# Keys turned by VectorE and moved by DMA, and two chunks in one score run, in a fused transformer block

## The chip, the cores and the metric

The kernel runs on one core of a Trainium2 chip. The metric is the device time of one execution, in microseconds (us). All arithmetic is in float32. The names used below: TensorE (PE) multiplies matrices and writes to PSUM, VectorE (DVE) and ScalarE (ACT) work on elements, GpSimd (POOL) does some element work in SBUF, SyncE (SP) issues nearly all DMAs.

## The reference, cut to what matters

x is 2 x 2048 x 256. Six modulation rows come from silu(c) and a matrix. Then, per token:

```
h = layernorm(x) * (1 + ca) + sa
q, k, v = split(h @ W_attn + b)              # 16 heads of 16 channels
phi(z) = exp(z @ omega - |z|^2 / 2) / sqrt(128)   # 128 features, z scaled by 1/4
S_t = sum over s <= t of phi(k_s) v_s^T ;  Z_t = sum over s <= t of phi(k_s)
y_t = phi(q_t) S_t / (phi(q_t) Z_t + 1e-6)   # causal linear attention
x = x + ga * (y @ W_proj + b_proj)
h = layernorm(x) * (1 + cb) + sb
x = x + gb * FFN(h)     # 4 experts, top 2, one shared base and a rank-4 part each
```

## The kernel before

**Tiles.** The 4096 tokens are eight blocks of 512 (`N = 8`, four per batch row). A block has four head groups g of four heads j and four chunks t of 128 tokens. Attention inside a chunk is a masked product of features; across chunks a running state `S[g]` carries the sums.

**Features.** `query_key` projects one 128-channel quarter n (0, 1 queries; 2, 3 keys), adds the bias on VectorE into `qs`, squares it on ACT, and SP writes both halves to DRAM (`qd`). `reload` reads one group's four heads back as `f`. `features` multiplies f by omega in four 32-row tiles (`pp`, four PSUM banks), `exponentials` makes `phi` on ACT, 128 features on the partitions and 512 tokens along the row, one tile for each head and side (side 1 is keys).

**Attention.** For every chunk the kernel does four things:

- `keys` turns the chunk's key features with four 128x128 transposes on TensorE (L413) into a PSUM bank `pk`; `keep_keys` copies the bank to SBUF (`kt`) on ACT (L421). `kt` has tokens on the partitions.
- `scores` (L431) makes the scores with 16 matmuls on 32-column groups of the array into the bank `pa`. The four matmuls of a round are of equal length and belong to four different heads (head j = c XOR u), so rows of `pa` hold blocks of 32 tokens in an order that depends on the head. VectorE multiplies the bank by `causal` into `am` (L437).
- `outputs` uses `kt` and v for the state's increment `ps` (L455, 16 matmuls), am and v for the part inside the chunk (L459) and S and phi for the part before it (L462). VectorE adds the increment to S (L471) and copies the 128x128 result to `y` (L475).
- Because of the order of tokens in `pa`, key features are written with their 32-token blocks exchanged (`quarters` in `exponentials`), and `values` computes v in 32-token pieces (L358), 64 instructions a chunk. v has 32 columns a head: 16 values and 16 ones, the ones giving the denominator.

**Order.** A loop runs over blocks i and eight pair steps k; step k handles two chunks. The written order of each engine is kept (`keep_written_order`), so what stands ahead of an instruction on its engine runs first. A step is: `run_full` (full-width TensorE work of other blocks), keys of two chunks, `scores` of the second chunk, `outputs` of the first, `features` of a later group, `amid` (VectorE work and DMAs of other blocks), exponentials, values, `scores` of the next step's first chunk, `outputs` of the second chunk, `behind`. `run_full`, `amid` and `behind` put the other stages of blocks i+1, i-1 and i-2 into fixed steps:

| step k | TensorE in run_full | VectorE and DMAs in amid and behind |
|---|---|---|
| 0 | channels1 (L283), hidden and first, query_key | divide_invert: den, rdr, inv |
| 1, 2 | hidden and first (L660, L646), query_key (L318), second (L646, g on L687) | step 2: divide (L515) |
| 3 | project (L522), its norm2_stats | norm2 (L273) |
| 4 | channels2 (L283), finish (L694) | |
| 5 | finish; router after scores | choose, norm1_stats |
| 6 | finish, low_rank (L618) | norm1 |
| 7 | weigh (L632, h on L637), finish, hidden and first, query_key, second | divide_load: den, num |

The FFN units (`hidden`, `first`, `second`) of a block begin in step 7 of the block after it and go on in steps 0 to 2 of the next, so they are missing in block 0 and in steps 0 to 2 of block 1, and the `finish` pieces are missing in blocks 0 and 1. The last block's FFN runs after the loop.

`divide_invert` writes the inverted denominators to DRAM (`rdr`, L503) and reads them back spread over partitions (`inv`, L506); `divide` multiplies num by inv; `project` needs its result. The SP queue issues its DMAs in the written order.

**PSUM.** Eight banks: `pa`, `pk`, `s` and five of the rotating tag `mm`.

Of the kernel before, what the change touches and what calls it, by code (L numbers as in the profile page):

```python
# [14 lines left out]
P = 128  # L15
NH = 16
# [16 lines left out]
def kernel(  # L33
# [32 lines left out]
    HW = 2 * DH  # L66
    CH = 8
# [91 lines left out]
    tri = work.tile([P, P], FP, tag="am", name="tri")  # L159
    make_upper_triangular(nc, tri, val=1.0, diag=True)  # L160
    causal = const.tile([P, HG, P], FP, name="causal")
    for c in range(4):
        for j in range(HG):
            nc.vector.tensor_copy(
                causal[c * CG : (c + 1) * CG, j, :], tri[(c ^ j) * CG : ((c ^ j) + 1) * CG, :]
            )

    pa = psum.tile([P, TB], FP, tag="pa", name="pa", bufs=1)
    nc.vector.memset(pa, 0.0)
# [144 lines left out]
    def query_key(i, n):  # L314
        s = st[i]
        pq = mm_tile(f"pq{i}_{n}")
        for k in range(KC):
            nc.tensor.matmul(  # L318
                pq, w_sb[:, k, n * P : (n + 1) * P], s["hT"][:, k, :],
                start=(k == 0), stop=(k == KC - 1),  # L320
            )


        tag = {1: "num", 3: "h2"}.get(n, "qs") if i == 0 else "qs"
        qs = work.tile(
            [P, 2, TB], FP, tag=tag, name=f"qs{i}_{n}", bufs=2 if tag == "qs" else 1
        )
        nc.vector.tensor_scalar(  # L328
            qs[:, 0, :], pq, bqk[:, n : n + 1], 1.0 / math.sqrt(DH), ALU.add, ALU.mult
        )  # L330
        nc.scalar.activation(qs[:, 1, :], qs[:, 0, :], AF.Square)
        qd = dram.tile([2 * HG, 2, DH, TB], FP, tag="qd", name=f"qd{i}_{n}", bufs=4)
        nc.sync.dma_start(qd[:, 0], qs[:, 0, :])
        if i == 0:
            nc.scalar.dma_start(qd[:, 1], qs[:, 1, :])
        else:
            nc.sync.dma_start(qd[:, 1], qs[:, 1, :])
        s["qd"][n] = qd

    def reload(i, n, hf):  # L340
        side, g = divmod(2 * n + hf, NG)
        f = work.tile([P, TB], FP, tag=f"f{side}{g}", name=f"f{i}_{side}{g}", bufs=1)
        nc.sync.dma_start(f, st[i]["qd"][n][hf * HG : (hf + 1) * HG].rearrange("j s d t -> (j s d) t"))
        st[i]["feat"][side, g] = f

    def values(i, t):

        s = st[i]
        if t == 0:
            s["v"] = work.tile([P, NT, NH, HW], FP, tag="v", name=f"v{i}")  # L350
            nc.gpsimd.memset(s["v"][:, :, :, DH:HW], 1.0)
        pv = mm_tile(f"pv{i}_{t}")
        wv = w_sb[:, :, 2 * C : 3 * C].rearrange("p k (g j d) -> p k j g d", j=HG, d=DH)
        for j in range(HG):
            for k in range(KC):
                for c in range(4):
                    t0 = t * P + (c ^ j) * CG
                    nc.tensor.matmul(  # L358
                        pv[c * CG : (c + 1) * CG, j * HG * DH : (j + 1) * HG * DH],
                        s["hT"][:, k, t0 : t0 + CG], wv[:, k, j],  # L360
                        start=(k == 0), stop=(k == KC - 1),
                    )
        nc.vector.tensor_add(
            s["v"][:, t, :, 0:DH].rearrange("p (g j) d -> p j g d", j=HG),
            pv[:, 0:C].rearrange("p (j g d) -> p j g d", j=HG, d=DH),
            bv_bc[:].rearrange("p (g j d) -> p j g d", j=HG, d=DH),
        )


    S, phi, turned, staged, y = {}, {}, {}, {}, {}  # L370

# [12 lines left out]
    def quarters(ap, j):  # L384

        n, b = {1: (2, CG), 2: (2, 2 * CG), 3: (4, CG)}[j]
        return ap.rearrange("p (a n b) -> p a n b", n=n, b=b)

    def exponentials(i, g, side, pps):
        for j in range(HG):  # L390
# [3 lines left out]
            if side and j:  # L394

                nc.scalar.activation(  # L396
                    quarters(ph[:], j)[:, :, ::-1], quarters(pps[j][:], j), AF.Exp, bias=lnm
                )
            else:
                nc.scalar.activation(ph, pps[j], AF.Exp, bias=lnm)  # L400
# [6 lines left out]
    def keys(i, g, t, bank=None):  # L407

        if not carried(i, t):
            return  # L410
        pk = bank or psum.tile([P, TB], FP, tag="pk", name=f"pk{i}_{g}{t}", bufs=1)
        for j in range(HG):
            nc.tensor.transpose(  # L413
                pk[:, j * P : (j + 1) * P], phi[i, g, 1, j][:, t * P : (t + 1) * P], ident
            )
        turned[i, g, t] = pk

    def keep_keys(i, g, t):
        if (i, g, t) in turned:
            kt = work.tile([P, HG, M], FP, tag="kt", name=f"kt{i}_{g}{t}")  # L420
            nc.scalar.copy(kt[:].rearrange("p h m -> p (h m)"), turned[i, g, t])  # L421
            turned[i, g, t] = kt

    def scores(i, g, t):

        q, k = ([phi[i, g, side, j] for j in range(HG)] for side in range(2))
        ts = slice(t * P, (t + 1) * P)
        for u in range(4):
            for c in range(4):
                j, t0 = c ^ u, t * P + c * CG  # L430
                nc.tensor.matmul(  # L431
                    pa[c * CG : (c + 1) * CG, j * P + u * CG : (j + 1) * P],
                    k[j][:, t0 : t0 + CG], q[j][:, t * P + u * CG : (t + 1) * P],
                    start=True, stop=True,
                )
        am = work.tile([P, HG, P], FP, tag="am", name=f"am{i}_{g}{t}")
        nc.vector.tensor_mul(am, pa[:].rearrange("p (h q) -> p h q", h=HG), causal)  # L437
        staged[i, g, t] = am

    def outputs(i, g, t):  # L440

        ts = slice(t * P, (t + 1) * P)
        am, kt = staged.pop((i, g, t)), turned.pop((i, g, t), None)
        fresh = i % NBLK == 0 and t == 0
        bank = psum.tile([P, TB], FP, tag="s", name=f"ps{i}_{g}{t}", bufs=1)
        ps, py = (bank[:, n * P : (n + 1) * P] for n in range(2))
        vs = [st[i]["v"][:, t, g * HG + j, :] for j in range(HG)]
        rows = [slice(j * HW, (j + 1) * HW) for j in range(HG)]  # L450
        if kt is not None:
            for j in range(HG):
                for c in range(4):
                    cg = slice(c * CG, (c + 1) * CG)
                    nc.tensor.matmul(  # L455
                        ps[cg, rows[j]], kt[:, j, cg], vs[j], start=True, stop=True
                    )
        for j in range(HG):
            nc.tensor.matmul(py[rows[j], :], vs[j], am[:, j, :], start=True, stop=fresh)  # L459
        if not fresh:  # L460
            for j in range(HG):
                nc.tensor.matmul(  # L462
                    py[rows[j], :], S[g][:, rows[j]], phi[i, g, 0, j][:, ts],
                    start=False, stop=True,
                )
        if kt is not None:
            new = work.tile([P, P], FP, tag=f"S{g}", name=f"S{i}_{g}{t}")
# [5 lines left out]
        if t == 0:  # L473
            y[g] = work.tile([P, TB], FP, tag="y", name=f"y{i}_{g}")
        nc.vector.tensor_copy(y[g][:, ts], py)  # L475
        if t == NT - 1:
# [254 lines left out]
    for n, hf in ((2, 0), (0, 0), (2, 1), (0, 1)):  # L731
        reload(0, n, hf)
    query_key(0, 3)
    query_key(0, 1)
    for n, hf in ((3, 0), (1, 0), (3, 1), (1, 1)):
        reload(0, n, hf)
# [4 lines left out]
    for g, side in ((0, 1), (0, 0)):  # L741
        exponentials(*features(0, g, side))
    keys(0, 0, 0)
    keep_keys(0, 0, 0)
    scores(0, 0, 0)
    exponentials(*features(0, 1, 1))
# [47 lines left out]
    def amid(i, k):  # L794
# [9 lines left out]
        if a < N:  # L804
            for kk, n, hf in (
                (1, 2, 0), (1, 2, 1), (2, 0, 0), (2, 0, 1), (3, 3, 0), (4, 3, 1), (7, 1, 0), (7, 1, 1),
            ):
                if kk == k:
                    reload(a, n, hf)
# [24 lines left out]
    def chunk_at(n):  # L834
        i, n = divmod(n, NG * NT)
        return i, *divmod(n, NT)

    TOTAL = N * NG * NT
    for i in range(N):
        for k in range(PAIRS):  # L840
            n = (i * PAIRS + k) * 2
            run_full(i, k)
            keys(*chunk_at(n + 1))
            if n + 2 < TOTAL:
                keys(*chunk_at(n + 2), bank=mm_tile(f"pk{n + 2}"))
            keep_keys(*chunk_at(n + 1))
            scores(*chunk_at(n + 1))
            if k == 5 and i:
                router(i - 1)
            outputs(*chunk_at(n))  # L850

            gi, gg = divmod(n // NT + 1 + k % 2, NG)
            quad = features(gi, gg, k % 2) if gi < N else None
            amid(i, k)
            if n + 2 < TOTAL:
                keep_keys(*chunk_at(n + 2))
            if quad:
                exponentials(*quad)
            if 3 <= k < 7 and i + 1 < N:
                values(i + 1, k - 3)  # L860
            if n + 2 < TOTAL:
                scores(*chunk_at(n + 2))
            outputs(*chunk_at(n + 1))
# [8 lines left out]
    def other_set(name):  # L872
        return [pa, mm_tile(f"{name}0")] + [
            psum.tile([P, TB], FP, tag=tag, name=f"{name}{tag}", bufs=1) for tag in ("pk", "s")
        ]
# [89 lines left out]
```

## Time and profile before

| | us |
|---|---|
| median of 3 runs (838.94, 842.99, 842.58) | 842.58 |
| span of the profiled execution, first to last instruction | 844.1 |
| PE busy | 785.1 |
| DVE busy | 420.3 |
| ACT busy | 296.8 |
| POOL busy | 134.5 |

The profiled execution is known by its span alone; the span is 1.5 us above the median of the runs. TensorE's mean granted clock was 0.968 of full speed; it was 0.80 from 25 to 50 us, 0.86 from 50 to 100 us, 0.86 again from 150 to 175 us and from 725 to 775 us, and 1.00 nearly everywhere between. Block 0 runs from about 43 to 110 us, block 1 to 193 us, and a later block takes 93 to 97 us.

How to read a page: the busy row gives the time in which an engine had an instruction under way. The chain is followed back from the last instruction to whatever released it, so its shares are of time on the path. In the timeline each row has the start, the length, the engine, the line, the operation, its output and inputs, the shape and the number of instructions; square brackets give idle time before it and what ended it. SPq rows are DMA issues on SP; their length is the time that issuing takes.

### The profile page before, as it was taken

How to read it: one execution, taken by the hardware profiler on the slowest of the kernel's cores; microseconds unless marked ns; L12 is line 12 of the kernel's file. 1: busy time of each engine (PE TensorE's matmuls, PEld its weight loads, DVE VectorE, ACT ScalarE, POOL GpSimd, SP SyncE). 2: the span in 40 equal slices, each digit the busy share in tenths (PEclk: the TensorE clock that was granted, in tenths of full speed). 3: DMA queues.
4: the chain of work that ended last, by engine and by line, in shares of the span. 5: the costliest groups of instructions: out<-in, count | busy, mean ns of one | idle time of the engine just before them, and what ended most of it. 6: DMA issues, size and time to landing. Idle time of an engine off the chain costs nothing.

```text
span 844.1 us, 34168 instructions
## 1 busy us (share of the span) xinstructions
PE 785.1 (93%) x15536; PEld 576.6 (68%) x15536; DVE 420.3 (50%) x1183; ACT 296.8 (35%) x570; POOL 134.5 (16%) x170
## 2 busy tenths in 40 slices
PE   4898999699999999999998999999899999889888
PEld 3466667566687667766776667776677677767666
DVE  5445467644557337544556347553464335532622
ACT  1354344334434343334433344334433233311021
POOL 1000200021201122021201122021220121012223
PEclk9798899989999999999999999999999999979999
DMA  3565235104410353013500353013410220102000
GB/s 120 180 207 188 97 118 177 42 4 136 143 42 16 98 158 91 16 50 113 158 28 16 92 164 89 17 37 121 118 50 16 75 69 14 53 2 66 1 26 26
DMA packets 45392, 68.18 MB, mean 81 GB/s; under 512 B 6848, under 2 KB 20352, under 8 KB 45248
## 3 DMA queue, kind: packets, MB, share of 16 engines
q1 hardware_dynamic: 43088, 63.90, 24.3%
q8 instruction: 122, 2.00, 1.0%
q10 hardware_dynamic: 2160, 2.10, 0.8%
q14 instruction: 22, 0.18, 0.1%
HBM read 36.37 MB, written 29.62 MB: 78 GB/s over the span
## 4 chain that ended last, share of the span: by engine, by line
PE 85%; DVE 9%; issue 3%; DMA 2%; POOL 0%; ACT 0%; SPq 0%; DVEq 0%; ACTq 0%; POOLq 0%
PE ph L660 12%; PE pa L431 10%; PE pf L694 9%; PE pp L378 8%; PE pk L413 7%; PE pq L318 6%; PE ph L646 4%; PE ps L455 4%; PE ps L459 4%; PE pv L358 4%; PE po L522 4%; PE ps L462 3%; PE pf L715 2%; PE ptf L283 1%; PE pl L618 1%
## 5 line engine op out<-in xcount | busy, mean ns | idle before, releaser
L688 POOL TENSOR_TENSOR g<-g,r 128x256 f32<-128x256 f32 x128 | 90.2, 736 | 372.0 <-DVE g L687 372.0
L437 DVE TENSOR_TENSOR am<-pa,causal 128x512 f32<-128x512 f32 x128 | 88.2, 689 | 72.4 <-PE pa L431 69.0
L400 ACT ACTIVATE phi<-pp,lnm 128x512 f32<-128x512 f32 x160 | 99.5, 688 | 61.4 <-PE pp L378 61.4
L421 ACT COPY kt<-pk 128x512 f32<-128x512 f32 x120 | 69.6, 581 | 146.0 <-PE pk L413 101.5
L431 PEld LDWEIGHTS pa<-phi,phi 128*32 128x32 f32 x4096 | 87.9, 113 | 37.8 <-DVE y L475 19.7
L660 PE MATMUL ph<-h,wi_sb 128*128 128x256 f32 x448 | 105.3, 388 | 4.8 <-DVE h L637 2.6
L694 PE MATMUL pf<-wo_g,g 128*128 128x256 f32 x448 | 103.3, 384 | 0.2 <-DVE g L687 0.2
L431 PE MATMUL pa<-phi,phi 128*32 128x64 f32 (+3 forms) x4096 | 101.1, 241 | 0.7 <-DVE am L437 0.7
L660 PEld LDWEIGHTS ph<-h,wi_sb 128*128 128x128 f32 x448 | 84.4, 193 | 22.0 <-DVE h L637 3.8
L694 PEld LDWEIGHTS pf<-wo_g,g 128*128 128x128 f32 x448 | 83.1, 190 | 17.2 <-issue 7.0
L328 DVE TENSOR_SCALAR qs<-pq,bqk 128x512 f32<-128x512 f32 x32 | 24.0, 750 | 132.5 <-PE pq L318 66.4
L378 PE MATMUL pp<-f,om 32*128 32x512 f32 x512 | 79.5, 660 | 2.5 <-DVE statsa L263 2.5
L674 ACT ACTIVATE r<-ph 128x256 f32<-128x256 f32 x112 | 34.1, 389 | 128.7 <-PE ph L646 119.4
L413 PE MATMUL pk<-ident,phi 128*128 128x128 f32 x480 | 69.1, 289 | 0.5 <-DVE qs L328 0.5
L413 PEld LDWEIGHTS pk<-ident,phi 128*128 128x128 f32 x480 | 58.2, 149 | 16.4 <-issue 12.7
L455 PE MATMUL ps<-v,kt 128*32 128x32 f32 x3840 | 60.7, 200 | 6.8 <-issue 6.5
L318 PE MATMUL pq<-hT,w_sb 128*128 128x512 f32 x128 | 63.6, 623 | 0.8 <-DVE hT L286 0.7
L459 PE MATMUL ps<-am,v 128*32 128x128 f32 x1024 | 60.3, 288 | 0.9 <-DVE y L475 0.7
L396 ACT ACTIVATE phi<-pp,lnm 128x512 f32<-128x512 f32 x96 | 58.7, 688 | 0.0
L462 PE MATMUL ps<-phi,S 128*32 128x128 f32 x960 | 55.5, 278 | 3.2 <-issue 3.2
L455 PEld LDWEIGHTS ps<-v,kt 128*32 128x32 f32 x3840 | 49.9, 113 | 7.7 <-issue 7.6
L687 DVE SCALAR_TENSOR_TENSOR g<-ph,rho 128x256 f32<-128x256 f32 x112 | 39.4, 414 | 25.8 <-PE ph L646 25.8
(175 smaller groups left out, 868.7 us busy)
## 6 DMA issues: line engine op xcount, KB each, us to landing
f<-qd SPq DMA_DIRECT2D x64, 256.0 KB
qd<-qs SPq DMA_DIRECT2D x60, 256.0 KB
ydr<-y SPq DMA_DIRECT2D x32, 256.0 KB
num<-ydr SPq DMA_DIRECT2D x16, 256.0 KB
inv<-rdr SPq DMA_DIRECT2D x16, 256.0 KB
xt<-in_x_dram SPq DMA_DIRECT2D x7, 512.0 KB
out_dram<-xt SPq DMA_DIRECT2D x7, 512.0 KB
wo_g<-in_woT_dram SPq DMA_DIRECT2D x2, 1024.0 KB
```

What stands on the lines that cost most here:

```text
L318: nc.tensor.matmul(pq, w_sb[:, k, n * P : (n + 1) * P], s["hT"][:, k, :], start=(k == 0), stop=(k == KC - 1),)
L378: nc.tensor.matmul(pp, om[rs, :], f[rs, :], start=True, stop=True, tile_position=(2 * DH * j, 0))
L400: nc.scalar.activation(ph, pps[j], AF.Exp, bias=lnm)
L413: nc.tensor.transpose(pk[:, j * P : (j + 1) * P], phi[i, g, 1, j][:, t * P : (t + 1) * P], ident)
L431: nc.tensor.matmul(pa[c * CG : (c + 1) * CG, j * P + u * CG : (j + 1) * P], k[j][:, t0 : t0 + CG], q[j][:, t * P + u * CG : (t + 1) * P], ...
L437: nc.vector.tensor_mul(am, pa[:].rearrange("p (h q) -> p h q", h=HG), causal)
L455: nc.tensor.matmul(ps[cg, rows[j]], kt[:, j, cg], vs[j], start=True, stop=True)
L459: nc.tensor.matmul(py[rows[j], :], vs[j], am[:, j, :], start=True, stop=fresh)
L462: nc.tensor.matmul(py[rows[j], :], S[g][:, rows[j]], phi[i, g, 0, j][:, ts], start=False, stop=True,)
L660: nc.tensor.matmul(ph, wi_sb[:, k, f * P : (f + 1) * P], s["h2"][:, k, ts], start=(k == 0), stop=False, skip_group_check=True,)
L688: nc.gpsimd.tensor_add(g, g, r[j // 2][:, j % 2, :])
L694: nc.tensor.matmul(po[:, 0:C], s["g"][f][:, t * P : (t + 1) * P], wo_g[i // NBLK][:, f, :], start=(f == 0), stop=(f == NF - 1),)
```

## The change

- TensorE no longer turns the keys. For every group of a block, `turn_keys` runs four VectorE transposes of 128x512, each of which turns 32x32 blocks, into `kb` (one buffer), and 16 DMAs within SBUF (32 partitions x 4 x 512 bytes, 64 KB each) that put the blocks together into `kt`. `pk` is gone, and with it `keep_keys` on ACT. It is called in even steps, after the exponentials of the group's queries, for the group whose increments begin two steps later; for the very first group before the loop.
- `scores` does both chunks of a pair in one run of 32 matmuls into two banks `pa0` and `pa1`; the even chunk has its 32-token blocks in order, the odd chunk in reverse (mirrored), so that each column group gets long and short matmuls in turn and 160 columns a head in all. The order no longer depends on the head: `quarters` goes, `causal` has two planes, and `values` is two full-width matmuls a chunk. `mirror_values` makes a copy of the odd chunks' v with the blocks in reverse (`vr`), four DMAs a block, issued in step 6.
- v has 17 columns a head (`DV`), and so has the state. A step now runs: `run_full`, values, `increments` of both chunks, S on VectorE, `scores` of the next pair, `outputs` of both chunks (y copied by ACT, 128x256), `features`, exponentials, `turn_keys` in even steps, `amid`, one `reload`, `behind`.
- `qs` has one buffer where it had two, and f four where it had eight.

```diff
-        qs = work.tile(
-            [P, 2, TB], FP, tag=tag, name=f"qs{i}_{n}", bufs=2 if tag == "qs" else 1
-        )
+        qs = work.tile([P, 2, TB], FP, tag=tag, name=f"qs{i}_{n}", bufs=1)
...
+    def quad_at(n):
+        i, n = divmod(n, 2 * NG)
+        return i, n // 2, 1 - n % 2
+
+    def reload(n):
+        i, g, side = quad_at(n)
+        if i >= N:
+            return
+        m, hf = divmod(side * NG + g, 2)
+        f = work.tile([P, TB], FP, tag="f", name=f"f{i}_{side}{g}", bufs=4)
+        nc.sync.dma_start(f, st[i]["qd"][m][hf * HG : (hf + 1) * HG].rearrange("j s d t -> (j s d) t"))
+        st[i]["feat"][side, g] = f
...
         pv = mm_tile(f"pv{i}_{t}")
+        for k in range(KC):
+            nc.tensor.matmul(
+                pv[:, 0:C], s["hT"][:, k, t * P : (t + 1) * P], w_sb[:, k, 2 * C : 3 * C],
+                start=(k == 0), stop=(k == KC - 1),
+            )
...
+    def mirror_values(i):
+        s = st[i]
+        s["vr"] = work.tile([P, NT // 2, NH, DV], FP, tag="vr", name=f"vr{i}")
+        odd = s["v"][:].rearrange("p (a e) h d -> p a e (h d)", e=2)[:, :, 1]
+        for c in range(4):
+            nc.sync.dma_start(
+                s["vr"][c * CG : (c + 1) * CG].rearrange("p a h d -> p a (h d)"),
+                odd[(3 - c) * CG : (4 - c) * CG],
+            )
...
+    def turn_keys(i, g):
+        blocks = work.tile([P, NT * 4, HG, CG], FP, tag="kb", name=f"kb{i}_{g}", bufs=1)
+        for j in range(HG):
+            nc.vector.transpose(
+                blocks[:, :, j, :], phi[i, g, 1, j][:].rearrange("p (b t) -> p b t", t=CG)
+            )
+        kt = work.tile([P, NT, 4, HG, CG], FP, tag="kt", name=f"kt{i}_{g}")
+        src = blocks[:].rearrange("p (t q) j m -> p t q (j m)", q=4)
+        for q in range(4):
+            for m in range(4):
+                nc.sync.dma_start(
+                    kt[q * CG : (q + 1) * CG, :, m].rearrange("p t j m -> p t (j m)"),
+                    src[m * CG : (m + 1) * CG, :, q],
+                )
+        turned[i, g] = kt
+
+    def scores(i, g, u):
+        q, k = ([phi[i, g, side, j] for j in range(HG)] for side in range(2))
         for j in range(HG):
+            for e in range(2):
+                t0 = (2 * u + e) * P
+                for c in range(4):
+                    a = 3 - c if e else c
+                    nc.tensor.matmul(
+                        pa[e][c * CG : (c + 1) * CG, j * P + a * CG : (j + 1) * P],
+                        k[j][:, t0 + a * CG : t0 + (a + 1) * CG],
+                        q[j][:, t0 + a * CG : t0 + P],
+                        start=True, stop=True,
+                    )
+        for e in range(2):
+            am = work.tile([P, HG, P], FP, tag="am", name=f"am{i}_{g}{u}{e}", bufs=3)
+            nc.vector.tensor_mul(
+                am, pa[e][:].rearrange("p (h q) -> p h q", h=HG),
+                causal[:, e, :].unsqueeze(1).to_broadcast([P, HG, P]),
+            )
+            staged[i, g, 2 * u + e] = am
+
+    def increments(i, g, u):
+        bank = py_bank
+        kt = turned[i, g]
...
+                    nc.tensor.matmul(
+                        bank[c * CG : (c + 1) * CG, (e * HG + j) * DV : (e * HG + j + 1) * DV],
+                        kt[:, t, c, j, :], st[i]["v"][:, t, g * HG + j, :],
+                        start=True, stop=True,
+                    )
...
+        nc.scalar.copy(y[g][:, 2 * u * P : 2 * (u + 1) * P], bank[:, 2 * P : 4 * P])
...
             run_full(i, k)
-            keys(*chunk_at(n + 1))
-            if n + 2 < TOTAL:
-                keys(*chunk_at(n + 2), bank=mm_tile(f"pk{n + 2}"))
-            keep_keys(*chunk_at(n + 1))
-            scores(*chunk_at(n + 1))
+            if 3 <= k < 7 and i + 1 < N:
+                values(i + 1, k - 3)
+            increments(*pair_at(n))
+            if n + 1 < TOTAL:
+                scores(*pair_at(n + 1))
             if k == 5 and i:
                 router(i - 1)
-            outputs(*chunk_at(n))
...
+            outputs(*pair_at(n))
+            gi, gg, side = quad_at(n + 3)
+            if gi < N:
+                exponentials(*features(gi, gg, side))
+                if side == 0:
+                    turn_keys(gi, gg)
             amid(i, k)
...
```

## The prediction

> **What bounds the kernel now.** I read the page's first section, then its chain of waits, then the chain in order of time and the engines' timelines for the third of a block's eight pair steps.
>
> ```profile
> PE 785.1 (93%) x15536; PEld 576.6 (68%) x15536; DVE 420.3 (50%) x1183; ACT 296.8 (35%) x570; POOL 134.5 (16%) x170
> ...
> PE 85%; DVE 9%; issue 3%; DMA 2%; POOL 0%; ACT 0%; SPq 0%; DVEq 0%; ACTq 0%; POOLq 0%
> PE ph L660 12%; PE pa L431 10%; PE pf L694 9%; PE pp L378 8%; PE pk L413 7%; PE pq L318 6%; PE ph L646 4%; PE ps L455 4%; PE ps L459 4%; PE pv L358 4%; PE po L522 4%; PE ps L462 3%; PE pf L715 2%; PE ptf L283 1%; PE pl L618 1%
> ```
>
> TensorE ends the kernel: 85% of the chain, and the key transposes (pk, L413) are 7% of it. VectorE's 50% looks like room, but that is an average. The next two views are one step, first the chain, then what VectorE and TensorE do at its end:
>
> ```profile
> 410.51 0.65 PE ph L646 x8
> 411.15 1.02 PE pk L413 x8
> 412.18 0.69 PE pa L431 x32
> 412.87 0.28 PE ps L455 x25
> 413.15 0.32 PE ps L459 x8
> 413.47 1.07 PE pp L378 x8
> 414.54 0.69 PE pa L431 x32
> ...
> 416.00 3.65 PE po L522 x16
> ```
>
> ```profile
> 411.27 1.41 DVE L687 SCALAR_TENSOR_TENSOR g<-ph,rho 128x256 f32<-128x256 f32 x4
> ...
> 412.94 0.69 DVE L437 TENSOR_TENSOR am<-pa,causal 128x512 f32<-128x512 f32 x1 [0.27 <-PE pa L431]
> ...
> 413.95 1.83 DVE L515 TENSOR_TENSOR num<-num,inv 128x512 f32<-128x512 f32 x2
> ...
> 415.93 0.48 PE L522 MATMUL po<-wp_g,num 128*128 128x256 f32 x1
> ```
>
> The division (L515) ends at 415.78 and the projection that reads it starts at 415.93: here VectorE is on time by 0.15 us, with nothing to spare. Last, the SP queue, the start of the kernel and a block's first steps, and one row of its waits:
>
> ```profile
> 1.24 1.88 SPq L95 DMA_DIRECT2D xt<-in_x_dram  x4
> ...
> 389.01 0.60 SPq L333 DMA_DIRECT2D qd<-qs  x1
> 389.66 0.60 SPq L337 DMA_DIRECT2D qd<-qs  x1
> 391.40 0.32 SPq L503 DMA_DIRECT2D rdr<-den  x1
> 397.33 1.27 SPq L506 DMA_DIRECT2D inv<-rdr  x2
> ```
>
> ```profile
> SPq L506 <- DMA rdr<-den: 28.8, 8, 5.8
> ```
>
> Issuing one DMA holds SP for 0.32 to 0.65 us, four alike are 0.47 us apart (1.88/4), and SP waits on average 3.6 us (28.8/8) for rdr before inv, with everything behind it in line.
>
> **What it takes away.** 480 transposes, eight a step at 1.02 us: 480/8 x 1.02 = 61 us, all on the path. With them go ACT's 120 copies (69.6 us) and VectorE's 128 y copies (35.8 us; ACT now makes 64); ACT and these copies are off the path, worth nothing by themselves. TensorE's small waits for pk and its copies (0.2 to 0.5 us at 306.8, 363.1, 375.3) also go: about 0.6 us in each of seven blocks, 4 us. Gain: 65 us.
>
> **What stays equal.** Scores: 16 matmuls take 0.58 us from start to start (the 128x512 features give another rate, 1.07/512 x 320 = 0.67). A pair runs 640 columns per column group in both kernels; between a saving of 0.1 and a loss of 0.18 a step I take 0, as the nearest row is the same matmul. Values: 64 instructions at 0.92 us become 4 full-width ones; the projection's like pieces take 3.65/4 = 0.91. Increments stream 17 columns, not 32, but the router's matmuls with 20 columns (0.62 us for 64 instructions) are no faster per instruction than these (0.28 for 32): 0.
>
> **What it adds.** 128 VectorE transposes of 128x512, four in every even step (0, 2, 4, 6). No row shows one. Bounds: 0.60 us, the pitch of the am rows, and 1.25, twice that; I take 0.69, am's own duration (88.2/128), the nearest operation of that size: 2.76 us a group. 512 DMAs of 64 KB within SBUF, 16 a group, all on SP: 0.34 to 0.62 us apart by the rows above; I take 0.47, 7.5 us a group. Both sit, in their engine's order, ahead of the division, the inversion's DMAs and the next step's qd. Where that shows, step by step:
>
> (a) Step 2 into 3. VectorE from the start of L646: g done at 2.24; two S adds 0.4; two am, now both behind the whole score run, 1.22: 3.86; transposes 6.62; division 1.75: 8.4. TensorE reaches the projection after 0.65 + 0.56 (increments, two of 0.28) + 1.16 (scores, two of 0.58) + 1.05 (outputs, two of 0.22 and 0.30) + 1.07 (features) = 4.5. New stall 3.9 us, in 7 blocks: 27.
>
> (b) Step 3 into 4: the second norm's xh pieces now follow both am; 0.6 us x 7 = 4.
>
> (c) Steps 0 to 2, the SP queue. From the end of step 0's transposes: key DMAs 7.5, rdr 0.3, its wait 3.6, inv 1.3, f 0.4, then step 1's two qd 1.3: 14.4; qd lands some 2.5 later (f at 400.61 waited about so long): 16.9. qs has one buffer now, so step 2's qs on VectorE waits for that landing, and behind it queue g, S, am, transposes and the division. Cover: rest of step 0 2.1, step 1 10.7 (3.65 + 0.65 + 1.91 + 0.65 + 3.84), step 2 up to qs 6.2, less the 4.2 that VectorE needs from the scores to the transposes' end: 14.8. Late by 2.1, in blocks 2 to 6: 10.
>
> (d) Block 1 has no FFN units in steps 0 to 2, so its cover is some 9 us shorter at the throttled clock (0.86): about 9 of stall. In step 7, transposes, norm1 and h x pw (4.2 + 1.3 + 1.3) meet TensorE after 3.2 (no finish in between): 3.6. The router's chain, with the same cover missing, 1. Sum 14.
>
> (e) Block 0 is shortest, 6 to 7 us a step. The first keys need 7.5 + 2.5 us of DMA at the start: 2.4 not covered. Each later group needs 4.2 + 7.5 + 2.5 = 14.2 against 2.1 + 6.5 + 2.3 = 10.9: 3.3, three times. In step 2 qs also waits for a qd that stands behind key DMAs and eight weight loads (6 us from 48.65): about 10. Less some 4 us of waits for weights that the old kernel has here too: 18.
>
> **What else moves, at nothing.** y's copy on ACT (0.39, as the 128x256 r rows) runs under the features (1.07), before the next increments write that bank. The exponentials, now last in a step, free four banks in some 2.8 us while the next step's first 3.65 us need one bank per 0.9; without that cover, up to 1.7 a step. The four mirror DMAs a block stand behind step 6's keys and have step 7 (over 11 us) to land. The reloads, one a step, are issued two steps ahead. The other even steps fall on finish (3.65 us) or hidden (3.65), which cover 2.76 us of VectorE; without that cover they would cost up to 2.76 each. Costs 27 + 4 + 10 + 14 + 18 = 73, against 65: plus 8. The profiled execution spanned 844.1 us, 1.5 above the median of 842.58; 844.1 + 8 - 1.5 is about 850.
>
> **Two rules of the Trainium skill.** The trace has no VectorE transpose. "VectorE: DVE Perf Modes", section "The three transpose paths", gives 311 ns for VectorE on a 128x128 bf16 tile and advises TensorE for full 128x128 transposes. Four such would be 1.24 us for 128x512, an estimate from that page; (a), (c), (d) and (e) would then rise to the slow rival's sum. "DMA: Bandwidth & Descriptors", section "Measured (HBM→SBUF, 128 partitions, SWDGE, issued from GpSimd)", gives 0.95 us for 64 KB; if the key DMAs ran one after another at that, a group would take 15 us and (c) would be 7.7 us worse. No run here shows either.
>
> **Rivals.** Faster, about 823: VectorE takes 0.60 and SP issues every 0.33 us, as for one contiguous tile (f, ydr at 0.32). Then (c) is gone (7.5 - 5.3 = 2.2), (a) is 25, (d) 11, (e) about 9, (b) 4: 49 against 65, and a score run that saves 0.1 us a step adds 6: 844.1 - 22 = 822. It decides below a pitch of 0.34. For it: rows of 0.32; against: kt's pattern has three levels on both sides, and such rows take 0.39 to 0.60.
>
> Much slower, about 890: one transpose takes 1.25, so a group 2.2 us more: (a) +15, (c) +11, step 7 +13, blocks 0 and 1 +15: near 905; or the pitch is 0.62, as for qd and inv, 2.4 us more a group: (c) +12, blocks 0 and 1 +12: near 875. From one transpose of 0.8 us on, step 7 is no longer covered. Against: am and hT, of the same size, take 0.69 and 0.81.
>
> That the transposes stay on TensorE is no rival: none is left in the new program.
>
> **Numbers.** Forecast 850 (its own range 836 to 870), 0.48; about 823 (800 to 838), 0.36; about 890 (870 to 920), 0.16. The range of 8 in 10 leaves out the low end of the second and the high end of the third: 810 to 893. A measurement of this kernel can tell about 0.5% from no change, 838.4 to 846.8. Faster 0.36 (nearly all of the second case); within 0.12 (mostly the forecast's low side); slower 0.52.
>
> **What would show it.** Right: PE's busy time down by 50 to 65 us; VectorE's up to 470 to 500; a row "PE po <- DVE num" of some 25 us where it was 3.0; VectorE's qs waiting for DMA qd<-qs; increments in block 0 waiting for kt; a transpose row near 0.69 us; SP at 0.45 to 0.5 us per kt DMA. Wrong: those waits missing with the rows short (faster), or score runs well over 1.3 us a pair, which none of my cases has.

## The result and the profile after

The changed kernel takes 935.36 us in the median (931.53 to 939.99), the kernel before 842.12 on the same chip: a ratio of 1.108, interval 1.100 to 1.116. The profiled execution spans 934.4 us with a mean granted clock of 0.907, where it was 844.1 and 0.968. The forecast was 850 and the top of its range 893. Some executions of a kernel are slower at a lower granted clock; the ratios leave these out and the medians do not, which is why 900.37 us below goes with a ratio of 1.060.

The page's busy row and its chain of waits, of the changed kernel:

```profile
PE 762.0 (82%) x13136; PEld 532.9 (57%) x13136; DVE 446.4 (48%) x1174; ACT 253.8 (27%) x514; POOL 128.3 (14%) x170
...
PE 48%; DVE 16%; SPq 15%; DMA 13%; issue 5%; ACT 1%; DVEq 0%; POOL 0%; ACTq 0%
SPq L424 12%; DMA qd<-qs 9%; PE ph L687 9%; PE pf L721 8%; PE pp L395 5%; DVE kb L417 4%; PE po L549 4%; PE pa L438 3%; DVE g L714 3%; PE py_bank L493 3%; PE pq L322 3%; PE ph L673 2%; PE py_bank L496 2%; PE py_bank L462 2%; PE pf L742 2%
```

TensorE carried 85% of the chain and now carries 48%. Its first line is no matmul: it is SP issuing the key DMAs (L424, 12%), then the landing of qd (9%). TensorE is idle for 934.4 - 762.0 = 172 us, where it was 59.

Next, two group rows (instructions, busy time, mean ns of one, idle time ahead) and three rows of waits (us, times, longest), of the changed kernel:

```profile
L330 DVE TENSOR_SCALAR qs<-pq,bqk 128x512 f32<-128x512 f32 x32 | 24.0, 751 | 226.9 <-DMA qd<-qs 151.8
...
L417 DVE STREAM_TRANSPOSE kb<-phi 128x512 f32<-128x512 f32 x128 | 79.4, 677 | 2.2 <-ACT phi L406 2.2
```

```profile
DVE qs L330 <- DMA qd<-qs: 151.8, 12, 21.4
...
PE py_bank L493 <- DVE S L478: 82.0, 26, 11.0
...
PE po L549 <- DVE num L542: 8.1, 8, 2.6
```

VectorE's turning costs what was taken for it (0.677 us, forecast 0.69). The large row is qs waiting for the transfer that still reads its one buffer. TensorE does not show that wait under its own name: it waits for S, which stands behind qs in VectorE's order. The stall that was forecast to be dearest, the projection behind the division, is the 8.1.

One such wait from end to end. First SP's timeline of block 4, steps 0 to 2, of the changed kernel, then the chain over the same time:

```profile
463.11 11.67 SPq L424 DMA_DIRECT2D kt<-kb  x16
474.88 1.75 SPq L530 DMA_DIRECT2D rdr<-den  x1
477.79 1.32 SPq L533 DMA_DIRECT2D inv<-rdr  x2
479.17 0.44 SPq L353 DMA_DIRECT2D f<-qd  x1
479.71 0.61 SPq L335 DMA_DIRECT2D qd<-qs  x1
480.42 0.61 SPq L339 DMA_DIRECT2D qd<-qs  x1
```

```profile
477.79 0.64 SPq L533
478.49 0.63 SPq L533
479.17 0.44 SPq L353
479.71 0.61 SPq L335
480.42 8.98 DMA qd<-qs
...
490.19 1.41 DVE g L714 x4
...
493.35 2.48 DVE kb L417 x4
495.83 0.58 DVE num L542
496.46 5.96 PE po L549 x16
```

Sixteen issues take 11.67 us; behind them stand the inversion and step 1's qd, which lands (has arrived, so that its source is free) at 489.40, 8.98 us after the start of its issue. VectorE starts qs at 489.52, after 18.07 us of idling, and then works off what is queued behind it: g, S, am, transposes, division. The projection follows at 496.46 and takes 5.96 us where it took 3.65. The landing itself, by windows of the changed kernel (length, busy us of PE, PEld, DVE, ACT and POOL, granted clock, DMA share, GB/s):

```profile
474.90:480.40 5.50, 5.50 (x129) 3.19 (x131) 0.00 (x0) 1.21 (x4) 0.00 (x0) 1.00 0.23 66
480.40:489.40 9.00, 0.67 (x38) 0.50 (x28) 0.00 (x0) 0.00 (x0) 0.00 (x0) 0.70 0.77 232
```

In nine microseconds TensorE works for 0.67. The DMA engines are busy: 9.0 us x 232 GB/s is 2.1 MB, the transfers that SP lets go at once. In this stretch the mean clock granted is 0.70; in windows of it, it is 1.00 up to 482 us, while TensorE still has work, and 0.64 from 482 to 489.

Where in the kernel the time went: from step 0 of one block to step 0 of the next (the start of the first hT on VectorE), blocks 0 to 5 took 67.8, 82.0, 94.3, 92.7, 97.3 and 94.6 us before, and 90.7, 109.2, 101.1, 106.7, 105.1 and 105.2 after. Blocks 0 and 1 lose 23 and 27 us, later blocks 7 to 14.

### The profile page after: what moved, and what is told of

The parts are those of the page before. It is cut to its first block, busy times and chain, and to the rows that moved or that the text cites. A ratio compares the mean times of both kernels' runs of the same rounds, so it can differ in the third digit from the quotient of the medians.

```text
span 934.4 us, 29993 instructions
## 1 busy us (share of the span) xinstructions
PE 762.0 (82%) x13136; PEld 532.9 (57%) x13136; DVE 446.4 (48%) x1174; ACT 253.8 (27%) x514; POOL 128.3 (14%) x170
## 2 busy tenths in 40 slices
DMA packets 121667, 103.74 MB, mean 111 GB/s; under 512 B 15552, under 2 KB 96640, under 8 KB 121536
## 4 chain that ended last, share of the span: by engine, by line
PE 48%; DVE 16%; SPq 15%; DMA 13%; issue 5%; ACT 1%; DVEq 0%; POOL 0%; ACTq 0%
SPq L424 12%; DMA qd<-qs 9%; PE ph L687 9%; PE pf L721 8%; PE pp L395 5%; DVE kb L417 4%; PE po L549 4%; PE pa L438 3%; DVE g L714 3%; PE py_bank L493 3%; PE pq L322 3%; PE ph L673 2%; PE py_bank L496 2%; PE py_bank L462 2%; PE pf L742 2%
## 5 line engine op out<-in xcount | busy, mean ns | idle before, releaser
L438 PE MATMUL pa<-phi,phi 128*32 128x128 f32 (+3 forms) x4096 | 96.8, 245 | 9.1 <-issue 9.1
L721 PEld LDWEIGHTS pf<-wo_g,g 128*128 128x128 f32 x448 | 84.8, 194 | 26.8 <-issue 11.4
L493 PE MATMUL py_bank<-am,v 128*17 128x128 f32 x512 | 31.1, 299 | 82.9 <-DVE S L478 82.0
L502 ACT COPY y<-py_bank 128x256 f32<-128x256 f32 x64 | 23.7, 371 | 250.9 <-PE py_bank L496 225.4
L395 PE MATMUL pp<-f,om 32*128 32x512 f32 x512 | 87.6, 736 | 5.1 <-DVE xha L277 4.7
L438 PEld LDWEIGHTS pa<-phi,phi 128*32 128x32 f32 x4096 | 85.0, 116 | 11.5 <-issue 9.9
L417 DVE STREAM_TRANSPOSE kb<-phi 128x512 f32<-128x512 f32 x128 | 79.4, 677 | 2.2 <-ACT phi L406 2.2
L462 PEld LDWEIGHTS py_bank<-v,kt 128*32 128x32 f32 x3840 | 44.4, 114 | 49.7 <-issue 37.1
L462 PE MATMUL py_bank<-v,kt 128*32 128x17 f32 x3840 | 52.7, 189 | 22.8 <-DMA kt<-kb 22.8
L496 PE MATMUL py_bank<-phi,S 128*17 128x128 f32 x960 | 58.0, 296 | 8.9 <-issue 8.9
L493 PEld LDWEIGHTS py_bank<-am,v 128*17 128x17 f32 x512 | 12.0, 100 | 89.5 <-DVE S L478 89.4
L333 ACT ACTIVATE qs<-qs 128x512 f32<-128x512 f32 x32 | 20.2, 632 | 147.4 <-DVE qs L330 147.4
```

The source lines that it names most:

```text
L395: nc.tensor.matmul(pp, om[rs, :], f[rs, :], start=True, stop=True, tile_position=(2 * DH * j, 0))
L417: nc.vector.transpose(blocks[:, :, j, :], phi[i, g, 1, j][:].rearrange("p (b t) -> p b t", t=CG))
L438: nc.tensor.matmul(pa[e][c * CG : (c + 1) * CG, j * P + a * CG : (j + 1) * P], k[j][:, t0 + a * CG : t0 + (a + 1) * CG], q[j][:, t0 + a * ...
L462: nc.tensor.matmul(bank[c * CG : (c + 1) * CG, (e * HG + j) * DV : (e * HG + j + 1) * DV], kt[:, t, c, j, :], st[i]["v"][:, t, g * HG + j, :],
L496: nc.tensor.matmul(py[rows[j], :], s0[:, cols[j]], phi[i, g, 0, j][:, t * P : (t + 1) * P], start=False, stop=True,)
L721: nc.tensor.matmul(po[:, 0:C], s["g"][f][:, t * P : (t + 1) * P], wo_g[i // NBLK][:, f, :], start=(f == 0), stop=(f == NF - 1),)
```

## The experiments

Medians are of several runs; each ratio is to the kernel before in the same session. That kernel's median lay between 842 and 848 us from one session to another, so ratios are compared where the runs are of different sessions. One per cent is 8.4 us.

**One transfer in place of sixteen.** The exchange of blocks is left out: the increments read blocks that were not put together.

```diff
-        for q in range(4):
-            for m in range(4):
-                nc.sync.dma_start(kt[q * CG : ...], src[m * CG : ...])
+        nc.sync.dma_start(kt[...], blocks[...])      # 1 MB, contiguous
```

> The 16 DMAs of 64 KB that put a group's keys together become one DMA of 256 KB from kb to kt: the same bytes and the same wait for the transposes, one issue on SP in place of 16. It leaves out the exchange of blocks between partitions, so the keys that the increments read are in the wrong order. Queue theory (SP is held some 11 us a group, the qd behind it lands late, and qs with its one buffer stops VectorE): VectorE's wait for DMA qd<-qs falls from 152 us to under 30, the increments' wait for kt goes, and the time to 840-865. VectorE rival (the transposes delay the division and what follows): at most 20 us less, above 910. Score-run rival (the new order of scores, increments and outputs is itself slow): no change, above 920.

(The transfer carries 1 MB, not the 256 KB of that text.) Measured: 842.85 us, ratio 0.995 (0.992 to 0.998). The sixteen issues in place of one make 1.108 - 0.995 = 11.3%, 95 us. The one transfer is also of another form, contiguous: the program's DMA packets fall from 121,667 to 52,542, so this run alone does not tell the number of issues from the form. That qd's landings are nearly as long with one transfer as with sixteen (see the landing, below) speaks for the issues.

**The same, and no turning.** The transposes are left out too; the one transfer moves a constant tile.

```diff
-            nc.vector.transpose(blocks[:, :, j, :], phi[i, g, 1, j]...)
+        blocks = fixed[0]      # written once
```

> As the run with one DMA, and the four VectorE transposes of each group are left out too: kb is filled once with a constant, and the key DMA no longer waits for VectorE. It leaves out the turning of the keys altogether. Against the run with one DMA it prices the transposes alone. Queue theory with my step (a): 25 to 40 us less than with one DMA, at 805-835. VectorE rival: most of the whole loss falls here, 70 us or more less than with one DMA. Score-run rival: stays above 880.

Measured: 814.85 us, ratio 0.960 (0.956 to 0.963). In one session with the run before: VectorE's turning costs 28.0 us. The new score runs are not what made the kernel slow.

**qd issued by ACT.**

```diff
-        nc.sync.dma_start(qd[:, 0], qs[:, 0, :])
+        nc.scalar.dma_start(qd[:, 0], qs[:, 0, :])
```

> Only the queue of the qd writes is changed: both halves are issued by ACT, so they no longer stand behind the 16 key DMAs on SP. Queue theory: VectorE's wait for qd falls below 40 us; the waits of the increments for kt and of the projection for the division stay, and ACT gets some 5 us of issuing a block; 870-895. If instead the landing (a burst of held transfers) and not the place in the queue makes qd late: 900-920. VectorE and score-run rivals: within 1% of 935.

Measured: 890.58 us, ratio 1.046 (1.039 to 1.053). With only qd out of the held queue, over half of the sixteen issues' loss is gone (6.2% of 11.3%). What remains shows in what SP still issues late; of this kernel's PE waits:

```profile
PE py_bank L459 <- DMA kt<-kb: 38.5, 25, 3.7
...
PE pp L392 <- DMA f<-qd: 10.4, 4, 3.7
```

**The division ahead of the transposes.**

```diff
-                if side == 0:
-                    turn_keys(gi, gg)
             amid(i, k)
+            if gi < N and side == 0:
+                turn_keys(gi, gg)
```

> Only the order is changed: a step's other VectorE work (division, inversion, norms) goes ahead of the four transposes, and the inversion's DMAs ahead of the key DMAs. VectorE rival and my step (a), with 25 to 30 us for the division behind the transposes: 905-912. Queue theory: the key DMAs start later by as much as the inversion's come earlier, so qd is hardly earlier, and the division is not what is waited for: 920-935.

Measured: 932.32 us, ratio 1.100 (1.096 to 1.103): under 1%. qs still waits 141.1 us for qd. While that wait ends last, VectorE's order behind it is nearly without effect.

**Keys turned by TensorE again, all else of the change kept.**

```diff
-            nc.vector.transpose(blocks[:, :, j, :], ...)
-        ... 16 DMAs a group
+                nc.tensor.transpose(pk[:, j * P : (j + 1) * P], phi[i, g, 1, j][:, t * P : (t + 1) * P], ident)
+            kt = work.tile([P, HG, M], FP, tag="kt", bufs=4)
+            nc.scalar.copy(kt[:].rearrange("p h m -> p (h m)"), pk)
```

> Everything of the change but the key turning stays (both chunks of a pair in one column run, the odd one mirrored, full-width values, 17-column state); the keys are turned by TensorE again, 4 transposes a chunk into a bank with one copy by ScalarE, and no key goes through a transfer. Theory (the loss is the SP queue's 16 key transfers a group and VectorE's turning, the rest of the change is a gain): SP is as free as before, no wait of qs for qd; against the run without any turning (814.85) TensorE gets back 480 transposes (61 us by the kernel before, less what now covers) and ScalarE's copies, so 840 to 875, and not above the kernel before by much. Rival (the score run or the one buffer for qs is itself slow): 880 and over, with waits of PE for am or of qs for qd still there.

Measured: 826.84 us, ratio 0.974 (0.970 to 0.978). It beats both kernels, by 2.6% and by 12%. Its busy row:

```profile
PE 777.0 (95%) x13616; PEld 557.6 (68%) x13616; DVE 375.0 (46%) x1046; ACT 317.3 (39%) x634; POOL 128.7 (16%) x170
```

**The same with two buffers for qs** (`bufs=2 if tag == "qs" else 1`, as in the kernel before).

> The faster form: keys turned by TensorE in the new structure, and qs with two buffers, since the turned blocks' tile is gone. Theory (the 15.4 us that VectorE's qs still waits for qd in the run with one buffer reach TensorE in part): 815 to 825 against 826.84. Rival (those waits are covered): the same 826 within 0.5%.

Measured: 825.92 us, ratio 0.980 (0.975 to 0.984). No difference from one buffer can be told: where SP is free, the wait of 15.4 us is covered.

**Neither turning nor transfer.** The increments read one constant tile.

```diff
+        kt = fixed[0]      # written once; no transposes, no key DMAs
```

> The changed kernel with the keys neither turned nor moved: the increments read one constant tile (the turning of the keys is left out). This is the floor of the new structure. Theory (the change's gain is the 61 us of transposes and little else, and the prediction's zeros for scores, values and increments hold): about 844 - 65 less the waits that remain, 780 to 800; against it the keys on TensorE (826.84) cost 27 to 47. Rival (the keys' turning on TensorE was partly hidden, or the new score run is dearer than the old): 805 to 815, as with the single transfer and no turning (814.85), so that one transfer of 1 MB a group costs nothing.

Measured: 796.32 us, ratio 0.947 (0.941 to 0.953). This is what is left when the turning costs nothing. In the same session TensorE's turning costs 825.92 - 796.32 = 29.6 us, half of the 61 of its instructions.

**Keys through DRAM, 5 issues a group.** Four transfers write the turned blocks to a scratch in DRAM, one reads them back in the next step.

```diff
+        for m in range(4):
+            nc.sync.dma_start(kd[:, :, :, m].rearrange("q p t c -> p t q c"), src[m * CG : (m + 1) * CG])
...
+            nc.sync.dma_start(kt[...], kd[...])      # one step later
```

> VectorE turns the keys as in the changed kernel, but its blocks go to a scratch in DRAM by 4 transfers after the transposes and come back by 1 transfer in the next step: 5 issues a group on SP in place of 16; the division's work comes ahead of the transposes. Theory (the number and form of the issues hold SP, not the bytes): SP is held some 3 us a group in place of 11.5, qs waits for qd at most 40 us in all, and the time lies near the run with one transfer (842.85), 835 to 860. Rival (the bytes, and the DMA engines that carry them in 512-byte packets, set the loss): over 890, as the bytes grow by another 32 MB and the packets stay as short.

Measured: 906.84 us, ratio 1.070 (1.065 to 1.075). A miss. SP was held as briefly as expected (3.2 to 4.5 us for the writes, 0.33 in the median for the read), and qs waited only 44.2 us for qd. But the increments now waited for the read; of this kernel's PE waits:

```profile
PE py_bank L470 <- DMA kt<-kd: 87.1, 21, 14.2
```

The read lands 4.8 to 10.2 us after its issue in the chain. Issue count alone did not make the transfer cheap, with its reader close behind. The time lies in the rival's range too, and this run does not tell the read's place from the added bytes.

**qs with two buffers, all sixteen transfers on SP** (one f fewer, single buffers for small tiles to make room).

> Only the buffers: qs has two again, paid for by one f fewer and single buffers for the router's small tiles, den and stats. The 16 key transfers stay on SP. Theory (the wait of VectorE's qs for qd is what turns the held queue into stall): the row qs <- qd falls from 151.8 us to under 40, and the time to 860 to 890, as when ScalarE issued qd (890.58); increments then wait more for kt, and features for a late f. Rival (the queue is simply late for everything, qd is only where it first shows): 915 to 940, the wait moves to features for f and increments for kt.

Measured: 888.53 us, ratio 1.046 (1.041 to 1.051); qs waits for qd once, 4.2 us, and the increments wait 34.9 us for kt, where it was 22.8:

```profile
PE py_bank L462 <- DMA kt<-kb: 34.9, 33, 7.1
...
DVE qs L330 <- DMA qd<-qs: 4.2, 1, 4.2
```

The one buffer costs 1.108 - 1.046 = 6.2%, 52 us. Block by block, measured as above, blocks 0 and 1 stay long (90.6 and 101.8 us), while blocks 2 to 4 take 93.6, 93.9 and 95.0, about as before the change. So the one buffer is paid for from block 1 on; block 0 loses as much with two.

**Key transfers issued by GpSimd** (`nc.gpsimd.dma_start`).

> The 16 key transfers of a group are issued by GpSimd in place of SP, all else is the changed kernel. Theory (it is SP's order that costs, not the transfers): qs <- qd falls below 40 us; POOL is held by the issues instead, 16 of about 0.6 to 1 us a group, ahead of its adds; 850 to 890. Rival (the transfers themselves, landing late, set it): increments wait for kt by over 60 us and the time stays at 915 or more.

Measured: 879.29 us, ratio 1.033 (1.025 to 1.041). The rows of the issues and of their landing (KB, median us from issue to landing), from this kernel's page:

```profile
L424 POOL DMA_DIRECT2D kt<-kb x512 | 278.8, 553 | 257.8 <-issue 126.2
...
kt<-kb POOLq DMA_DIRECT2D x512, 64.0 KB, 2.3
```

The same 512 transfers cost 63 us less when they do not stand in SP's line (7.5%: ratio 1.108 against 1.033). The program's packets fall too, to 64,323, at the same bytes, so the queue is not all that differs. Some 30 us remain against one transfer; in its trace the increments wait 31.6 us for kt.

**Ten and thirteen issues in place of sixteen.** Two of the four rows of blocks (or one) go as one contiguous transfer each, with no exchange of their blocks; the bytes stay.

```diff
         for q in range(4):
+            if q < 2:            # or q < 1
+                nc.sync.dma_start(kt[rows]..., blocks[rows]...)
+                continue
```

> Of the 16 key transfers of a group 8 stay, and the other 8 are put together into 2 contiguous ones without the exchange of blocks (that part of the computation is left out); the bytes are the same. SP is held some 8 x 0.65 + 2 x 0.4 = 6 us a group, under the prediction's 7.5. Theory (the prediction's account of the cover was right and only the time of one issue was mis-sized; about 10 us of time for each us of holding): 835 to 850, no more than with one transfer a group (842.85) by much, and qs <- qd under 50 us. Rival (no threshold: each us of holding costs 8 to 9 us from the first on): 885 to 895.

> As the run with ten, but 12 of the 16 key transfers stay and 4 are put into 1: SP is held some 12 x 0.65 + 0.4 = 8.2 us a group, just over the prediction's 7.5. Theory (threshold, then 10 us and more for each us): 855 to 875. Rival (a straight line from one transfer, 842.85, to sixteen, 935): 903 to 912.

Measured: 873.35 us with ten, ratio 1.036 (1.031 to 1.042), and 900.37 with thirteen, 1.060 (1.051 to 1.069). Neither the threshold nor the straight line: from 1 to 10 issues each adds 0.5% of the time, from 10 to 16 each adds 1.2%. SP's timeline, with ten:

```profile
447.58 1.29 SPq L425 DMA_DIRECT2D kt<-kb  x2
448.93 5.90 SPq L431 DMA_DIRECT2D kt<-kb  x8
454.87 0.59 SPq L353 DMA_DIRECT2D f<-qd  x1
```

The group takes 454.83 - 447.58 = 7.25 us here (7.1 to 9.5 over all groups, median 7.7), so this run holds SP for about the 7.5 us that the prediction took. It is 873, not 850, and VectorE's qs still waits for qd:

```profile
DVE qs L330 <- DMA qd<-qs: 97.1, 9, 17.9
```

Pitch was not the only error.

**xt two steps later.** The 512 KB load behind step 1's qd is moved to step 3.

```diff
-            if k == 1:
+            if k == 3:
                 load(i + 2)
```

> The changed kernel with one load moved: the 512 KB xt, issued by SP right behind step 1's qd, goes out two steps later. If the landing of qd takes 7 to 9 us because it shares the DMA engines with what is issued behind it (2.1 MB at 232 GB/s), it falls by about 512 KB / 232 GB/s = 2.2 us, in the five or six blocks that load one: the time falls by about 11 us, to 920 to 928. If the landing is a fixed latency or the issue order alone: 932 to 938.

Measured: 932.01 us, ratio 1.102 (1.094 to 1.110). The time lies at the lower end of the second expectation and cannot be told from 1.108. The landings decide: step 1's qd of blocks 3 to 6 landed after 7.79, 8.98, 7.10 and 6.79 us in the changed kernel, and after 7.41, 7.94, 7.61 and 8.03 here, no 2.2 us less. The xt behind it is not what makes qd land late. Whether the other transfers let go with it do, or the length is fixed, stays open.

**Ten issues and two buffers for qs.**

> Ten issues a group (8 exchanges and 2 contiguous pieces; part of the exchange of blocks is left out), as before held 7.5 us, and qs with two buffers (one f fewer, single buffers for the router's small tiles). If the landing of qd was the only other mis-sized term of the prediction's sum, its step (c) is gone altogether and the time is 850 - 10 = 840, within 835 to 848, about that of one transfer a group (842.85). If other terms were short too (features late for f, increments for kt, blocks 0 and 1): 855 to 870.

Measured: 846.32 us, ratio 1.009 (1.004 to 1.013). At about the predicted pitch and with the wait for qd taken away, the rest of the prediction's sum comes out in total, though not in its parts (below, under the gain). The four corners as ratios:

| | SP held about 7.5 us a group | about 11.5 us |
|---|---|---|
| qs with two buffers | 1.009 | 1.046 |
| qs with one buffer | 1.036 | 1.108 |

## Why the prediction was wrong

The direction (slower) was the likelier one of the forecast; the size was wrong by 85 us. Two terms were mis-sized, the pitch of the key issues and the landing of qd. Both stand in step (c), which had 10 us; the pitch also stands in (e), block 0, where the keys themselves come late. They come late in block 1 too (6.3 us of waits for kt), which (d) does not have.

**Step (c) in its own terms.** In block 4, shown above, from the first key issue to qd's landing is 489.40 - 463.11 = 26.3 us, where (c) had 16.9. The key issues take 11.8 for its 7.5; rdr, inv and f together 4.8 for its 5.6; the two qd with the landing 9.7 for its 3.8. That is 9.4 us later than reckoned. TensorE then idles 10.98 us for S, where (c) had 2.1.

**The pitch, a term mis-sized.** One issue of this pattern takes 0.60 us (median 0.599) and the next mostly starts 0.64 to 0.73 later. The prediction took 0.47, the pitch of whole-row loads, and had 0.62 as its upper bound, though it noted itself that rows of patterns with three levels take up to 0.60. That row was the nearest, and the gap to the next issue came on top. A group is 10.2 to 12.7 us, 11.4 in the median, not 7.5. The corners give the price of ten issues becoming sixteen: 1.108 - 1.036 = 7.2%, 61 us, with one buffer for qs, and 3.7%, 31 us, with two.

**The landing, a term mis-sized.** The prediction gave qd 2.5 us, from the row of f at 400.61. That row is no wait: it is the issuing of two f, 0.79 and 1.87 us long, and between 385 and 405 us no f waits for qd. The chain after, followed through each stretch of 100 us, has eleven landings of qd from 5.9 to 9.0 us and one of 1.0, and they take 5.9 to 7.6 with ten issues and 5.8 to 7.9 even with one key transfer a group. The trace of before had the evidence, in SP's own waits:

```profile
SPq L343 <- DMA qd<-qs: 71.2, 23, 4.9
```

f waited up to 4.9 us for a qd already issued, so a landing takes at least that. With 7 in place of 2.5, step (c) is late by 4.5 us more in each block even at the forecast's pitch. The runs agree: at about 7.5 us of holding, the second buffer is worth 1.036 - 1.009 = 2.8%, 23 us, where (c) had 10 in all. And 846 with that wait gone stands beside the 840 that the sum leaves without (c).

**The slope.** In the slow rival 2.4 us more of holding cost 24 us, 10 for each. With one buffer the 4 us from ten issues to sixteen cost 61, 15 for each; with two, 3.7%, 31 us, 8 for each. Blocks 0 and 1, where (d) and (e) had 14 and 18 us, less some 9 of gain each, came out 27 and 23 longer. (e) gave 10 us to a qd behind key DMAs and eight weight loads; that wait is 21.4 us in the trace after, but it is not what block 0 pays for. With two buffers it is gone, the increments' wait for kt in block 0 rises from 14.8 us to 23.5, and block 0 is as long (90.6 us against 90.7; 91.0 with qd issued by ACT). The pitch explains block 0 by (e)'s own sum for the keys: 2.4 + 3 x 3.3 = 12 at 7.5 us a group becomes 6.3 + 3 x 7.2 = 28 at 11.4, an estimate, beside 23 longer and 9 of gain.

**The clock.** The prediction priced a stall at its own length. The same 13,136 matmuls keep TensorE busy for 737.9 us with one transfer (granted clock 0.953), 743.0 with ten issues (0.943) and 762.0 in the changed kernel (0.907). How much of these 24 us is loss is not shown: with the division ahead of the transposes they take 773.6 (0.905), and the time is no longer. One stall shows the effect itself. Behind the landing above, the granted clock is 0.50 from 489 to 500.5 us and 1.00 again from 502.5; the projection there takes 5.96 us at a mean clock of 0.62, where it took 3.65 at 1.00 before.

**Steps and signs that held, and some that did not.** Turning on VectorE: 0.677 us each, 28 us for all of it, against (a)'s 27 and (b)'s 4. That agreement is partly luck: the wait that (a) is about, the forecast row "PE po <- DVE num" of some 25 us, is 15.2 with one transfer, and only 8.1 in the changed kernel, where the later wait for qd takes its place on the path. Two other signs failed. PE's busy time fell by 23 us and not by 50 to 65 (60 in the run with neither turning nor transfer); VectorE's rose to 446.4 and not to 470 to 500, although a transpose took the time that was forecast. Increments in block 0 do wait for kt (14.8 us from 40 to 130 us), VectorE's qs does wait for qd, and SP's pitch is that of the slow rival, or a little over it. The zeros for scores, values and increments held, taken together, in the steady blocks: with keys on TensorE these take 92 to 96 us, as before. At the start the new structure gains 8.5 us in block 0 and 5.0 in block 1, which the prediction did not have; why was not tried.

**The gain was over-stated.** 65 us were to come off; with the turning free of cost it is 5.3%, 45 us. Of the 4 us for small waits, three rows were named; they are 0.20 to 0.38 us long, and the trace puts two of them down to qs on VectorE, not to pk. TensorE's busy time did fall by 785.1 - 725.0 = 60, the forecast's 61, but its idle time rose from 59.0 to 67.8. It now waits 20.4 us for S on VectorE, a row that the kernel before does not have and the prediction put at nothing; shorter steps that cover less of VectorE's work would explain it, but that was not tried. The costs beside (c) were over-stated as well: 846.32 against this floor is 1.009 - 0.947 = 6.2%, 52 us, where the sum had 63. That 846 lies near the 840 is therefore partly luck.

**The rivals.** "Faster, about 823" needed a pitch of 0.33: with one issue a group the kernel is at 842.85, so even that would have given no such gain. "Much slower, about 890" had the right mechanism, a pitch of 0.62, and too small a price, 875.

**The rules of the Trainium skill.** "VectorE: DVE Perf Modes", section "The three transpose paths": its 311 ns for a 128x128 bf16 tile gave an estimate of 1.24 us for 128x512; the trace has 0.677 in float32, and the measurement decides. The page's advice to turn full 128x128 tiles on TensorE, where the result may go to PSUM, stands in its section "Rules for kernel authors" and holds here: 826.84 against 842.85 for VectorE even when a single issue carries the blocks. "DMA: Bandwidth & Descriptors", section "Measured (HBM→SBUF, 128 partitions, SWDGE, issued from GpSimd)": 0.95 us for 64 KB gave an estimate of 15 us a group one after another. The groups take 11.4 us in the median to issue on SP and 8.7 on GpSimd's queue (446.21 to 454.89 for one of them), where one lands in 2.3 us in the median, so they overlap.

## What to carry to other kernels

Work taken from a busy engine and given to DMAs was paid for here in the issuing queue. Count the issues, take the time of one from the row with the nearest pattern and add the gap, and list what stands behind them and which buffer waits for that. Cutting a buffer from two to one made no difference that could be told while the queue was free (826.84 against 825.92 us) and cost 52 us when it was held. For a transfer's landing, read who has waited for that very transfer, and make sure that the row is a wait. And when a large wait is found, look at the run without it, block by block: the 21.4 us in block 0 cost nothing of their own that could be told.

## What was not expected of the hardware

SP's time for one issue did not go by the bytes: 0.60 us in the median for 64 KB in 512-byte pieces, 0.47 to 0.54 for 1 MB in one contiguous transfer. Nor is it fixed for one pattern: an f of 256 KB takes 0.32 to 1.87 us in the kernel before (median 0.39) and 0.32 to 2.86 in the changed one (median 0.59); what the long ones wait for was not tried. And a TensorE that had stalled for 11 us got a lower clock for the work behind the stall: 0.50 for some 8 us, so that the projection, 3.65 us in the trace before, took 5.96.
